# New TensorE times in a statically planned four-layer network, layer 3's priorities kept per image, and a new set of plan parameters

## The chip, the core and the metric

The kernel runs on one core of a Trainium2 chip. Time is device time in microseconds (us) for one call. The core's engines work at once, each through its own instruction queue in order: TensorE (PE in the profile) multiplies matrices, VectorE (DVE) and ScalarE (ACT) do elementwise work, and the SP queue issues DMA transfers. PEld is the weight load of TensorE. GpSimd (POOL) does next to nothing here.

## What is computed

The input x is 8 images of 32 channels and 256 x 256 points, float32. Four residual layers follow one another, each behind a group normalisation over 16 groups:

```
x = x + L0(gn(x))   # 1x1 convolution; a 5x5 filter per channel pooled from its result; depthwise 5x5 convolution
x = x + L1(gn(x))   # quantised 3x3 "adder" convolution: out[o] = -sum over channels and taps of |q - w[o]|
x = x + L2(gn(x))   # ordinary 3x3 convolution, 32 to 32 channels, with bias
x = x + L3(gn(x))   # 8x8 windows: layer norm, three small KAN layers summed, a fourth KAN layer, plus the window
```

A KAN layer is a layer norm, eight Gaussians `exp(-((ln - grid_k) / denom)^2)` of every element, a matrix product with them, and a second product with `silu(x)`.

Layer 1 has no product form. The kernel writes |q - w| through max(q - w, 0): for every output channel and each of the 9 taps an elementwise pass gives max(q - w, 0), TensorE sums it over channels with a matrix of constants, and a total of q over all taps, one for each half image, mends the rest.

## The kernel before

**Tasks and the plan.** The kernel is not written in the order in which it runs. `stage0` to `stage3` describe each layer of each image as tasks (`Plan.add`): an engine, an assumed duration in us, the buffers it needs, and a rank, which is its priority. `Plan.run` plays these tasks through on the host with a list scheduler: whenever an engine is free it takes the ready task of the lowest rank whose buffers fit. The order that comes out is what each engine's queue gets. On the chip that order is fixed; an engine that meets a late operand waits, and all behind it waits too. Assumed durations and ranks therefore change nothing but the order, and the buffers' allocation.

**Layer 1 as filler.** Layer 1 of an image is 32 passes (2 halves of the image, 16 groups of 2 output channels, `Pass`), each of 18 terms (2 channels, 9 taps). One term has three steps: a distance (`Parts.distance`: L1202 on DVE, or a piece of it on ACT, L1204) of 32 rows of 256 or 258 points from `qh` into a bfloat16 buffer `dv`; a gather (`Parts.gather`: 16 matmuls at L1220, called a gather below) that adds it into the PSUM tile `psA`; and the release of the `dv` buffer. There are two `dv` buffers (`NDV = 2`). In image 0 alone distances may also lie in the big `arena`. `Pass.piece` lets ACT begin a term's first `RA` rows once ACT has had no other work for `IDLE[image]` us; what is left of the term is taken by DVE or by ACT. DVE takes a distance whenever none of its ordinary tasks is ready, and a gather is urgent on PE. At the end of a pass `Parts.residual` (L1212, L1214) adds layer 1's input, loaded into the tile `xr` by SP (L1294), and the half image's total `ss`; an ACT task (L1299, the gate) empties `psA` into `xr`, ACT squares it for the next norm (L730), and SP stores it (L1310). There is one `psA`, so the next pass's gathers wait for the gate. There are `NXR` tiles `xr`.

**Totals.** A half image's total is nine PE tasks of 16 matmuls (L1226) into `psC`, an ACT copy (L1270) and a DVE subtraction (L1274) into `ss`. Their rank is the image's number minus `SUMS`.

**The other layers in between.** While image b is in layer 1, its neighbours are in layers 0, 2 and 3. Layer 0 (from image 1 on) is matmuls at L1027, evicted by ACT at L1053; layer 2 is L1378. Layer 3 works through 8 chunks an image. Most of its PE work is the helper `mm16` (L687: 16 float32 matmuls, which the trace records as 32). Its ACT work is mostly the Gaussians: a square (L1636) and an exponential (L1651), 256 of each an image; its DVE work is the scaling by the norm (L1531). Once all of layer 1 is done (`Plan.over`), DVE may take squares (L1641), evictions (L1479) and squares of the variance (L1483) from ACT. All chains of layer 3 go through one PSUM tile `psB`. `TURN` holds 14 shifts of priority for the steps of layer 3; one row serves images 0 to 6, a second one image 7. `L0A`, `L0B`, `L2A`, `L3A` and `L3B` place each image's layers in the ranks.

**Fillers at the end.** After the last layer-1 work, `spin` matmuls (L1845) fill 0.7 of each idle stretch that the plan expects on PE.

Of the kernel before, what the change touches and what calls it, by code (L numbers as in the profile page):

```python
# [29 lines left out]
GRID = 8  # L30
# [32 lines left out]
WK = KG + 5  # L63
# [8 lines left out]
TURN = (  # L72
    (0.8482, -0.3, 0.2988, 1.0831, 0.6872, 0.2653, 0.143, 0.632, 0.405, 0.4783, 0.2467, 0.4067, 0.8418, 0.3135),
    (0.8722, -0.1754, 0.2988, 0.9706, 0.6706, 0.3621, 0.0629, 0.4997, 0.7442, 0.312, 0.2568, -0.197, 0.8314, 0.3104),
)
# [7 lines left out]
URGENT = 1  # L83
NXR = 1
NXO = 2
MEM = 41280
IDLE = (8.0, 8.0, 16.0, 8.0, 8.0, 8.0, 8.0, 8.0)
NDV = 2
SPARE = 2816
WIDE_SPARE = 5632  # L90
BASE_SPARE = 0
EARLY = 0
HOLDT = 2
HOLD = 1
SUMS = 1.667
RA = 16
HALVES = 0
WARM = 0.7
PAIR = 0
SWITCH = 0.006  # L100
L0A = (0.1812, 0.5892, 0.4534, 0.6, -0.0586, 0.2257, 0.2237)
L0B = (1.2, 1.2, 1.2, 1.2, 1.2, 1.2, 1.2)
L2A = (-0.1294, 0.3683, 0.0757, 0.4, 0.3872, 0.3266, 0.371, 0.2281)
L3A = (0.6, 0.5583, 0.6, 0.5465, 0.6, 0.6, 0.3101, 0.3024)
L3B = (0.5054, 1.4107, 0.3679, 0.499, 0.4628, 1.2444, 1.3823, 0.5913)

# [33 lines left out]
class Plan:  # L140
# [7 lines left out]
    def __init__(self, room):  # L148
        self.tasks, self.passes = [], []

        self.free, self.places, at = {}, {"psA": [0], "psB": [0], "psV": [0], "psC": [0], "dv": list(range(NDV))}, 0
        for kind, n, size in room:
            if size:
                self.places[kind] = list(range(n // size))
            else:
                self.free[kind] = [(at, n)]
                at += n
        self.first_pass, self.filling = 0, False

    def add(self, eng, us, fn, r=(), w=(), rank=0.0, after=(), table=None, spare=0, kb=0, acc=(), dma=(1, 4.0)):  # L160
        t = Task()
        t.eng, t.us, t.fn, t.rank, t.table, t.spare, t.kb = eng, us, fn, rank, table, spare, kb
        t.dma = dma
        t.n, t.gate, t.other = len(self.tasks), None, None
        deps = {d for d in after}
        for b in r:
            deps.update(b.writers)
        for b in w:
            deps.update(b.writers)
            deps.update(b.readers)  # L170
        t.need = [b for b in acc if b.kind != "fixed"]
        t.bufs = list({id(b): b for b in (*r, *w, *acc)}.values())
        for b in t.bufs:
            b.left += 1
            if b.first is None:
                b.first = t
                if b.kind != "fixed" and b not in acc:
                    t.need.append(b)
        for b in acc:
            b.writers.append(t)  # L180
        for b in r:
            b.readers.append(t)
        for b in w:
            b.writers, b.readers = [t], []
        t.wait = len(deps)
        t.outs = []
        for d in deps:
            d.outs.append(t)
        t.ready, t.over = 0.0, False
        self.tasks.append(t)  # L190
        return t
# [75 lines left out]
    def run(self):  # L267
# [24 lines left out]
        while left or any(not p.done for p in self.passes):  # L292
            moved = True
            while moved:
                moved = False
                for e in engines:
# [31 lines left out]
                    if e == "PE":  # L328
                        us += 0.05 * ((t.n is None) != self.filling)
                        self.filling = t.n is None  # L330
                    if t.table in (LN_EXP, SILU):
# [5 lines left out]
                    if e == "SP":  # L337
                        at, (n, land) = now, t.dma
                        for _ in range(n):
                            at = max(at, landed.pop(0)) + us / n  # L340
                            landed.append(at + land)
                        busy[e] = at
                        mover = max(mover, now) + t.kb / self.RATE
                        t.end = max(mover, at + land)
                        landed[-1] = t.end
                    else:
                        busy[e] = t.end = now + us
                        if e == "ACT" and t.n is not None:
                            self.idle = t.end
                    heapq.heappush(events, (busy[e], 1, count, None))  # L350
                    heapq.heappush(events, (t.end, 2, count, t))
                    count += 1
# [4 lines left out]
            while events and events[0][0] <= now + 1e-9:  # L357
# [3 lines left out]
                elif what == 2:  # L361
# [4 lines left out]
                    for d in t.outs:  # L366
                        d.wait -= 1
                        lat = 0.0 if d.eng == t.eng and t.eng != "SP" else self.LAT[t.eng]
                        d.ready = max(d.ready, t.end + lat)
# [17 lines left out]
    def filler(self, eng, us, fn, need, bufs, ended):  # L387
        t = Task()
        t.eng, t.us, t.fn, t.need, t.bufs = eng, us, fn, list(need), list(bufs)
        t.n, t.table, t.kb, t.outs, t.ended, t.rank = None, None, 0, [], ended, 0.0  # L390
        return t

# [25 lines left out]
class Pass:  # L418
# [61 lines left out]
    def on_pe(self, plan, urgent):  # L480
# [4 lines left out]
        if self.queue and (len(self.queue) >= URGENT or not urgent):  # L485
            o, t, d, a, z = self.queue.pop(0)
            us, bufs, n = 0.05 + 0.22 * (-(-z // 8) - a // 8), [d], 1
            for v in range(a // 2, z // 2):
                self.rows[v % NJ] += 1
            fn = lambda: self.parts.gather(self, d, o, t, a, z)  # L490
        elif (
            not self.added and self.residual.over and self.low.over and (self.left < 6 or not urgent)
            and self.whole()
        ):
            us, bufs, n = 1.6, [self.ss], 0
            fn = lambda: self.parts.residual(self)
# [17 lines left out]
def kernel(  # L514
# [178 lines left out]
    class Norm:  # L693
# [43 lines left out]
        def finish(self):  # L737
# [4 lines left out]
            def first():  # L742
# [11 lines left out]
            plan.add(  # L754
                "PE", 0.6, lambda: nc.tensor.matmul(pv(), mat(average), self.mv, start=True, stop=True),
                r=[small], w=[p], rank=self.rank,
            )

            def second():
# [6 lines left out]
            plan.add(  # L766
                "PE", 0.6, lambda: nc.tensor.matmul(pv(), mat(average), self.d, start=True, stop=True),
                r=[small], w=[p], rank=self.rank,
# [49 lines left out]
    def stage0(b, rank, span, after):  # L818
# [40 lines left out]
        def fold():  # L859
# [5 lines left out]
        plan.add(  # L865
            "PE", 0.6, lambda: nc.tensor.matmul(psC[:, 0, 0:1], mat(W0), mr, start=True, stop=True),
            r=[sm["c0"]], w=[p], rank=r(0.2),
# [11 lines left out]
        def parts():  # L879
# [11 lines left out]
        plan.add(  # L891
            "PE", 0.6,
            lambda: nc.tensor.matmul(pk(), mat(MS), part.rearrange("p i j -> p (i j)"), start=True, stop=True),
# [8 lines left out]
        plan.add(  # L902
            "PE", 0.6, lambda: nc.tensor.matmul(pk(), mat(W0), pooled, start=True, stop=True),
            r=[sm["c1"]], w=[p], rank=r(0.2),
# [83 lines left out]
        def one_block(k, half, xo):  # L988
# [59 lines left out]
            for t in [K + mid] + [t for t in range(3 * K) if t != K + mid]:  # L1048
                plan.add("PE", 0.98, lambda t=t: taps(t), r=[xt, sm["w4"]], w=[p], acc=[xo] if t == K + mid else [], rank=rk)
            plan.add("PE", 0.8, edge, r=[sm["diag"], sm["c1"]], w=[p], rank=rk)  # L1050
            prev.append(plan.add(
# [8 lines left out]
        for k in range(NCH):  # L1060
# [63 lines left out]
            for n, t in enumerate(tap_order):  # L1124
                plan.add(
                    "PE", 1.07, lambda t=t, n=n, tap=tap: tap(t, first=(n == 0)),
                    r=[xt, sm["diag"]], w=[p], rank=rk,
# [108 lines left out]
    def stage1(b, x1buf, qbuf):  # L1236
# [3 lines left out]
        for h in range(NH):  # L1240
# [24 lines left out]
            for t in range(9):  # L1265
                plan.add(
                    "PE", 0.88, lambda h=h, t=t: Parts().total(h, t), r=qh_buf, w=[p], rank=b - SUMS
                )
# [50 lines left out]
    def stage2(b, norm, x2buf, rank, span, after):  # L1319
# [15 lines left out]
        for k in range(NCH):  # L1335
# [51 lines left out]
            for n, t in enumerate(taps):  # L1387
                plan.add(
                    "PE", 1.07, lambda t=t, n=n, tap=tap: tap(t, first=(n == 0), last=(n == 8)),
                    r=[xt, sm["w2f"]], w=[p], rank=rk,  # L1390
# [31 lines left out]
    def stage3(b, norm, x3buf, rank, span):  # L1422
        im = img[b]
        odd, turns = b % 2, TURN[b == nb - 1]
        cenf, resf = (wt[:, K0 * K0 + 3 + 2 * odd + i, :] for i in range(2))
# [3 lines left out]
        def fold():  # L1429
# [8 lines left out]
        plan.add(  # L1438
            "PE", 0.6, lambda: nc.tensor.matmul(psC[:, 0, 0:1], mat(C32), mr, start=True, stop=True),
            r=[sm["c3", odd]], w=[p], rank=r(0),  # L1440
# [24 lines left out]
        def variance(n, t, cen, bias, rk, src, sq=None):  # L1465
# [3 lines left out]
            for p, ps, i, us in parts():  # L1469
                at = slice(i * FS, (i + (2 if us < 1 else 4)) * FS)  # L1470
                plan.add("PE", 0.87 + 0.2 * us, lambda ps=ps, i=i: cen(ps(), i), r=src, w=[p], acc=[c], rank=rk, spare=SPARE)
                evict = plan.add(
# [23 lines left out]

            plan.add("PE", 1.1, var, r=[sq], acc=[v], rank=rk)
            return c
# [13 lines left out]
        def scale(n, t, c, rk):  # L1512

            rs = stat[t][1]
            for p, ps, first, us in parts():
# [11 lines left out]

                plan.add("PE", 0.87 + 0.2 * us, bc, r=[rs, c], w=[p], rank=rk)
                plan.add(
# [72 lines left out]
        def kan(n, t, at, rk):  # L1602
# [20 lines left out]
            def main(k):  # L1623
                mains.append(plan.add(
                    "PE", 1.07,
                    lambda bas=bases[k]: mm16(psB, tl[:, WK + 9 * n + k, :], spans(sb(bas)), k == 0, False, view=view),
                    r=[bases[k]], w=[acc], rank=rk,
# [76 lines left out]
            if n == 3:  # L1704
# [6 lines left out]
            plan.add(  # L1711
                "PE", 1.07, lambda: mm16(psB, tl[:, WK + 9 * n + GRID, :], src, False, not more, view=view),
                r=[si], w=[acc], rank=rk,
            )
            for m, (a, wm, s_) in enumerate(more):
                plan.add(
                    "PE", 1.07, lambda wm=wm, s_=s_, m=m: mm16(psB, wm, s_, False, m == len(more) - 1),
                    r=[a, sm["resf", odd]], w=[acc], rank=rk,
# [249 lines left out]
```

## Time and profile before

| what | us |
|---|---|
| median of 3 runs | 14098.98 |
| lowest and highest of them | 14069.48 to 14101.82 |
| the profiled execution's own time | 14074.93 |
| its span, first to last instruction | 14073.2 |
| PE, DVE, ACT busy in it | 12345.7, 12645.1, 11273.3 |
| first distance, last gather (trace) | 404.5, 12615.1 |

The span falls into four stretches by the trace: a head until about 408 us (layer 0 of image 0), image 0's layer 1 without any layer 3 beside it until about 1640 us (the last time that a distance lies in the arena), seven more images of layer 1 with the other layers beside them until 12615 us, and a tail in which layers 2 and 3 of the last images run. Matmul records overlap, so a busy PE is not a full one; DVE and ACT records of neighbouring instructions overlap by about 0.1 us, so the step from one start to the next is the better cost.

### The profile page before, as it was taken

Reading aid. Unit: us, or ns where it says so; the run is one execution under the profiler, and the core shown is the slowest. Engines: PE = TensorE matmul, PEld = TensorE weight load, DVE = VectorE, ACT = ScalarE, POOL = GpSimd, SP = SyncE. Lnnn points to the kernel's source line nnn. Section 1 sums busy time; section 2 is a strip of 40 time slices with the busy share of each in tenths; the row PEclk is TensorE's granted clock in tenths of the full one; section 3 lists DMA queues with packets and bytes.
Section 4 is the critical chain, followed back from the end, with each engine's and each line's share of the span. In section 5 each row is a group of like instructions: output and inputs, shape, how many; then the busy total and the mean of one; then the engine's idle time right before and its main releaser. Section 6 shows DMA issues by size and latency. Waiting matters only on the chain. (4 is left out here: it accounts for less than half of the span.)

```text
span 14073.2 us, 508061 instructions
## 1 busy us (share of the span) xinstructions
PE 12345.7 (88%) x237500; PEld 4097.9 (29%) x237744; DVE 12645.1 (90%) x7707; ACT 11273.3 (80%) x7526; POOL 17.3 (0%) x23
## 2 busy tenths in 40 slices
PE   6798978999899888998899988998888888788888
PEld 4232322222222222222222222222222222223333
DVE  1899899998999999998989899898999999995787
ACT  1565568898688888888888888888889879997887
POOL 0000000000000000000000000000000000000000
PEclk9898999999999999999999999999999999999999
DMA  4434365665765655656666656665554545556675
GB/s 113 109 79 110 95 160 145 152 155 143 184 152 148 159 165 138 146 144 156 175 147 150 153 149 174 158 149 153 150 132 127 137 135 136 127 136 180 167 194 152
DMA packets 2259390, 2052.63 MB, mean 146 GB/s; under 512 B 1418240, under 2 KB 1897472, under 8 KB 2168192
## 3 DMA queue, kind: packets, MB, share of 16 engines
q1 hardware_dynamic: 2257280, 2020.11, 57.0%
q8 instruction: 1860, 30.47, 0.9%
q14 instruction: 250, 2.05, 0.1%
HBM read 1247.93 MB, written 771.75 MB: 144 GB/s over the span
## 5 line engine op out<-in xcount | busy, mean ns | idle before, releaser
L1202 DVE TENSOR_SCALAR dv<-qh,w1q 128x8192 bf16<-128x8192 bf16 (+6 forms) x4922 | 10122.0, 2121 | 492.4 <-PE psA L1220 476.8
L1220 PE MATMUL psA<-dv,sel_b 128*32 128x512 bf16 x70823 | 4861.2, 389 | 816.9 <-DVE dv L1202 676.1
L1636 ACT ACTIVATE arena<-arena,kb 128x2048 f32<-128x2048 f32 x1690 | 3351.7, 1997 | 360.9 <-DVE arena L1531 250.8
L1220 PEld LDWEIGHTS <-sel_b 128*32 128x32 bf16 x73728 | 1808.7, 96 | 5272.1 <-issue 4091.0
L1651 ACT ACTIVATE arena<-arena 128x2048 f32<-128x2048 f32 x1690 | 3191.0, 1902 | 0.4
L687 PE MATMUL psB<-arena,tl 32*32 32x512 f32 x67184 | 2558.0, 610 | 274.7 <-ACT arena L1651 134.2
L1027 PE MATMUL psC<-arena,w 64*32 64x510 f32 (+2 forms) x26880 | 1779.2, 599 | 34.2 <-issue 20.8
L687 PEld LDWEIGHTS psB<-arena,tl 32*32 32x32 f32 x67184 | 668.6, 104 | 1337.3 <-issue 666.2
L1531 DVE TENSOR_TENSOR arena<-psB,arena 128x2048 f32<-128x2048 f32 (+1 forms) x298 | 662.4, 2223 | 65.8 <-PE psB L1523 64.4
L1378 PE MATMUL psB<-arena,tl 32*32 32x510 f32 (+3 forms) x16384 | 625.4, 605 | 21.4 <-issue 21.1
L1027 PEld LDWEIGHTS psC<-arena,w 64*32 64x32 f32 x26880 | 366.7, 105 | 907.1 <-issue 866.0
L1204 ACT ACTIVATE dv<-qh,w1n 128x4096 bf16<-128x4096 bf16 (+2 forms) x95 | 349.5, 3697 | 325.6 <-PE psA L1220 313.1
L687 PE MATMUL psB<-si,tl 32*32 32x512 f32 x13952 | 574.8, 607 | 21.6 <-issue 8.1
L1724 ACT ACTIVATE si<-psB,cols_sb 128x2048 f32<-128x2048 f32 x185 | 363.2, 1963 | 272.0 <-PE psB L687 268.9
L1641 DVE SCALAR_TENSOR_TENSOR arena<-arena,kb 128x2048 f32<-128x2048 f32 x234 | 538.4, 2347 | 30.7 <-PE psB L687 21.0
L1474 ACT ACTIVATE arena<-psB 128x2048 f32<-128x2048 f32 (+1 forms) x216 | 402.8, 1865 | 195.4 <-PE psB L687 194.5
L1482 ACT ACTIVATE arena<-arena 128x2048 f32<-128x2048 f32 x286 | 547.4, 1914 | 11.7 <-DMA syd<-arena 4.1
L1651 ACT ACTIVATE arena<-arena,kbsq 128x2048 f32<-128x2048 f32 x234 | 455.4, 1993 | 0.8 <-DVE arena L1641 0.8
L1523 PE MATMUL psB<-rs,tl 32*32 32x512 f32 x9248 | 353.0, 615 | 97.4 <-DVE arena L1531 62.0
L1845 PE MATMUL psA<-qh,eye_b 128*128 128x512 bf16 x1636 | 395.5, 384 | 0.0
L1491 PE MATMUL psV<-arena,tl 128*32 128x512 f32 x2560 | 349.0, 615 | 51.1 <-ACT arena L1482 31.1
L1299 ACT ACTIVATE xr<-psA,wsum 128x512 f32<-128x512 f32 x256 | 174.0, 680 | 252.1 <-PE psA L1220 235.5
(194 smaller groups left out, 7507.1 us busy)
## 6 DMA issues: line engine op xcount, KB each, us to landing
arena<-x SPq DMA_DIRECT2D x192, 1024.0 KB
arena<-in_x_dram SPq DMA_DIRECT2D x450, 384.0 KB
arena<-y SPq DMA_DIRECT2D x128, 1024.0 KB
si<-sy SPq DMA_DIRECT2D x484, 256.0 KB
arena<-in_x_dram SPq DMA_DIRECT2D x256, 256.0 KB
xr<-x SPq DMA_DIRECT2D x256, 256.0 KB
x<-xr SPq DMA_DIRECT2D x256, 256.0 KB
x<-arena SPq DMA_DIRECT2D x64, 1024.0 KB
```

The lines of the kernel that those rows point to most:

```text
L687: nc.tensor.matmul(view(o[j * C : (j + 1) * C, i - first, :]), w_, src(rows, i, j), start=start, stop=stop)
L1027: nc.tensor.matmul(o[:, :, c0:c1], w4[rows, t, :], grid(rows)[:, 2 * j + y : 2 * j + y + 2, c0 + dx : c1 + dx], start=t == K + mid, stop=F ...
L1202: nc.vector.tensor_scalar(dst, src, w1q[:, at : at + 1], 0.0, ALU.subtract, ALU.max)
L1220: nc.tensor.matmul(psA[j * C : (j + 1) * C, :], sel_b[:, w, :], v, start=start, stop=stop)
L1378: nc.tensor.matmul(o[:, lo - 2 * j : hi - 2 * j, c0:c1], (wc if t == 4 else tl[:, W2T + t, :])[rows], d[rows, lo + dy + 1 : hi + dy + 1, c ...
L1474: lambda ps=ps, at=at: nc.scalar.activation(sb(c)[:, at], ps().rearrange("p s f -> p (s f)"), func, bias=shift),
L1482: square = plan.add("ACT", 1.82, lambda: nc.scalar.activation(sb(sq), sb(c), AF.Square), r=[c], w=[sq], rank=rk)
L1531: lambda ps=ps, at=at: nc.vector.tensor_tensor(sb(c)[:, at], ps().rearrange("p s f -> p (s f)"), sb(c)[:, at], ALU.mult),
L1636: lambda: nc.scalar.activation(sb(bas), sb(rb), AF.Square, bias=kb[:, n, k : k + 1]),
L1641: nc.vector.scalar_tensor_tensor(sb(bas), sb(rb), kb2[:, n, k : k + 1], sb(rb), ALU.add, ALU.mult)
L1651: lambda: nc.scalar.activation(sb(bas), sb(bas), AF.Exp, scale=-1.0, bias=0.0 if sq.eng == "ACT" else kbsq[:, n, k : k + 1]),
L1845: nc.tensor.matmul(psA, eye_b, qh[:, 0:2, 0:W], start=True, stop=True)
```

## The change

The change has three parts, all in what the plan is fed with; no engine instruction is new.

1. PE's assumed times. A task may now have a `lap`: it is taken off when the next PE task is of the same sort (ordinary or gather), and paid when the sort changes. Tasks of 16 float32 matmuls go from 1.07 to 1.07 with a lap of 0.187, layer 0's from 0.98 to 1.013 with 0.137, a gather of 32 rows from 0.05 + 4 x 0.22 to 0.113 + 4 x 0.216 with 0.105; the fixed 0.05 for a change of sort goes.
2. `TURN` has one row for each image.
3. New values: `NXR` 1 to 2, `IDLE`, `RA` 16 to 4, `SUMS`, `HOLDT`, `SPARE`, `WIDE_SPARE`, `SWITCH`, and all of `TURN`, `L0A` to `L3B`.

```diff
 TURN = (
-    (0.8482, -0.3, 0.2988, 1.0831, 0.6872, 0.2653, 0.143, 0.632, 0.405, 0.4783, 0.2467, 0.4067, 0.8418, 0.3135),
-    (0.8722, -0.1754, 0.2988, 0.9706, 0.6706, 0.3621, 0.0629, 0.4997, 0.7442, 0.312, 0.2568, -0.197, 0.8314, 0.3104),
+    (0.4936, -0.3, -0.0877, 0.9919, 0.4488, -0.3, 0.0124, 1.5, 0.1463, 0.6118, 0.5329, 0.0977, 0.7248, 0.4639),
...
+    (0.4384, -0.3, 0.1294, 0.698, 1.5, -0.1148, 0.0001, 0.581, 0.1183, 0.4505, 0.1448, 0.1669, 0.602, 0.3026),
 )
-NXR = 1
+NXR = 2
-IDLE = (8.0, 8.0, 16.0, 8.0, 8.0, 8.0, 8.0, 8.0)
+IDLE = (2.0, 16.0, 2.0, 8.0, 8.0, 1000.0, 8.0, 0.5)
-SPARE = 2816
-WIDE_SPARE = 5632
+SPARE = 3584
+WIDE_SPARE = 6656
-HOLDT = 2
+HOLDT = 1
-SUMS = 1.667
-RA = 16
+SUMS = 1.405
+RA = 4
-SWITCH = 0.006
-L0A = (0.1812, 0.5892, 0.4534, 0.6, -0.0586, 0.2257, 0.2237)
...
+SWITCH = 0
+L0A = (0.3978, -0.0952, -0.2956, -0.2968, -0.4814, -0.5, -0.4469)
...
                     if e == "PE":
-                        us += 0.05 * ((t.n is None) != self.filling)
-                        self.filling = t.n is None
+                        us += self.lap * ((t.n is None) != self.filling)
+                        self.filling, self.lap = t.n is None, t.lap
...
-                        busy[e] = t.end = now + us
+                        t.end = now + us
+                        busy[e] = t.end - t.lap
...
-            us, bufs, n = 0.05 + 0.22 * (-(-z // 8) - a // 8), [d], 1
+            us, bufs, n = 0.113 + 0.216 * (-(-z // 8) - a // 8), [d], 1
...
-                plan.add("PE", 0.98, lambda t=t: taps(t), r=[xt, sm["w4"]], w=[p], acc=[xo] if t == K + mid else [], rank=rk)
+                plan.add("PE", 1.013, lambda t=t: taps(t), lap=0.137, r=[xt, sm["w4"]], w=[p], acc=[xo] if t == K + mid else [], rank=rk)
...
-    odd, turns = b % 2, TURN[b == nb - 1]
+    odd, turns = b % 2, TURN[b]
```

## The prediction

> **What bounds the kernel now.** I read the page first: DVE is the busiest engine (90%), PE and ACT follow. An average over stages says little, so next came the busy times by stretch, then DVE's waits in the longest stretch, then the timeline where the waits are large.
>
> From the page, the span, the busy row and the costliest group:
>
> ```profile
> span 14073.2 us, 508061 instructions
> PE 12345.7 (88%) x237500; PEld 4097.9 (29%) x237744; DVE 12645.1 (90%) x7707; ACT 11273.3 (80%) x7526; POOL 17.3 (0%) x23
> L1202 DVE TENSOR_SCALAR dv<-qh,w1q 128x8192 bf16<-128x8192 bf16 (+6 forms) x4922 | 10122.0, 2121 | 492.4 <-PE psA L1220 476.8
> ```
>
> Distances alone are 10122 us of DVE. Busy by stretch (length, then PE, PEld, DVE, ACT, POOL, granted clock, DMA share, GB/s):
>
> ```profile
> 408.00:1640.00 1232.00, 1104.87 (x17680) 366.86 (x17706) 1218.87 (x817) 740.91 (x434) 4.58 (x2) 0.95 0.38 90
> 1640.00:12615.00 10975.00, 9714.78 (x189416) 3039.87 (x189625) 10271.52 (x6063) 9260.62 (x6308) 11.45 (x13) 0.98 0.59 149
> 12615.00:14073.00 1458.00, 1282.45 (x23434) 518.03 (x23422) 1078.90 (x600) 1197.82 (x722) 0.00 (x0) 0.98 0.67 175
> ```
>
> In image 0's layer 1 DVE is idle for 13 us of 1232: it is the bound, and ACT has 491 us to spare. In the seven images after it DVE is idle for 703 us of 10975 (6.4%), ACT for 1714. In the tail no engine is full; a chain of DVE, ACT, PE and `psB` sets the time. So before 12615 us a microsecond less of DVE work, or of DVE waiting, is about a microsecond less of time. What DVE waits for between 1640 and 12615 us (us in total, times, longest):
>
> ```profile
> DVE dv L1202 <- PE psA L1220: 474.1, 486, 22.9
> DVE ss L1274 <- ACT ss L1270: 71.4, 9, 25.2
> DVE tiny L723 <- ACT xr L1299: 54.9, 18, 24.5
> ```
>
> The first row is the pair of `dv` buffers: a distance waits until a gather has freed one. What held the gather shows in the timeline, at two places. At 8914 us (start, us, engine):
>
> ```profile
> 8913.78 2.35 DVE L1202 TENSOR_SCALAR dv<-qh,w1q 128x8192 bf16<-128x8192 bf16 x1
> 8931.06 0.69 DVE L1274 TENSOR_TENSOR ss<-psC,ss 128x512 bf16<-128x512 f32 x1 [14.94 <-ACT ss L1270]
> 8939.35 6.91 DVE L1202 TENSOR_SCALAR dv<-qh,w1q 128x8256 bf16<-128x8256 bf16 x3 [7.60 <-PE psA L1220]
> ...
> 8922.02 8.37 PE L1226 MATMUL psC<-qh,sel_b 128*32 128x512 bf16 x144
> ```
>
> All nine tasks of a total run as one block of 8.37 us, and DVE stands for 22.5 us: first at the subtraction behind it, then for a buffer. At 9394 us:
>
> ```profile
> 9416.71 9.18 DVE L1202 TENSOR_SCALAR dv<-qh,w1q 128x8256 bf16<-128x8256 bf16 x4 [22.88 <-PE psA L1220]
> ...
> 9401.79 0.68 SPq L1294 DMA_DIRECT2D xr<-x  x1
> ...
> 9412.17 1.12 PE L1212 MATMUL psA<-xr,mats_sb 128*128 128x512 f32 x2 [2.14 <-DMA xr<-x]
> ```
>
> The pass cannot close before its `xr` has landed, no gather of the next pass can run, and DVE stands for 22.9 us. There is one `xr`.
>
> **The change, part by part.**
>
> *Less distance work on DVE.* In the timeline at 900 us distances start 2.26 us apart for 8192 points and 1.19 for 4096, so one of n points costs 0.13 + 0.00026 n us. In the compiled order of both kernels DVE's distances fall from 5116 to 5037 and their points (for each partition) from 37,143,328 to 36,831,052; ACT's pieces rise from 172 to 361, points from 703,712 to 1,015,988. DVE saves 312,276 x 0.00026 + 79 x 0.13 = 81 + 10 = 91 us. Of the points 188,912 (49 us) leave in image 0, where DVE is 99% busy; 88,956 leave in image 2 and 62,072 in image 7; the others take a few back. All of it lies before 12615 us.
>
> What ACT gains: the trace has 3584 points at 3285 ns and 4096 at 3709, so 0.83 ns a point and, start to start, a fixed 0.2 us. 312,276 x 0.00083 + 189 x 0.2 = 297 us, of which 178 in image 0, where 491 are idle. The cover is that idle time; if it is gone, each us on ACT delays squares and exponentials, on which `psB`'s PE tasks wait. After image 0 ACT goes from 84% to about 85%. The ACT pieces of 1024 points (`RA = 4`) are not in this trace: from the rows 0.2 + 0.85 = 1.05 us; bounds 0.9 and 1.3.
>
> [...] The row gives DVE a fixed 0.13 us an instruction. [...]
>
> *Totals.* Before, six of the 14 totals after image 0 run as a block of eight or nine tasks; DVE's gaps from a total's first matmul to 9 us past its last are 31.8, 11.0, 7.6, 9.4, 14.5 and 22.5 us, 97 in all. The eight that are strewn between gathers have 25 us, 3.1 each. After, by the compiled order, none behind image 0 has more than three tasks in a row, and they start 1 to 8 terms into their half instead of 2 to 18. Six at 3.1: 97 - 19 = 78 us saved. What is late next is the subtraction L1274 itself, if ACT's copy comes late; that is in the 3.1.
>
> *Residuals.* With `NXR = 2` SP's queue has two loads of `xr` ahead of a store, where before load and store strictly alternate; the number of DMAs hardly changes (2398 to 2396 rows). PE's stretches without a gather around a residual that exceed 4 us (0.88 us a task) fall from 22 to 11 of 222, and their excess from 141 to 9 us. PE's waits for `xr` were 52 us (37 times); the DVE gaps beside them, outside the totals, add up to 38 us. I take the 38.
>
> *PE's assumed times.* The trace around 6005 us: a gather and an ordinary task alternate at 2.05 us the pair (0.98 and 1.07), and four L1027 in a row take 3.6, so 0.88 to 0.90 each. The old plan assumed 2.10 and, in a row, 1.07 or 0.98; the new one gives 2.05 and 0.88. This moves no cost by itself. Stretches of PE between gathers over 3.5 us, after image 0, lose 113 of 163 us of excess; that is totals and residuals again, so not counted twice. Two tasks between gathers become commoner (566 to 900 times), about 1.9 us, under one distance of 2.26. Bounds: -60 to +60 us, taken at 0.
>
> *Tail.* PE's tasks behind the last gather are the same in number. DVE gives 20 squares back (-45), takes 10 squares of the variance (+22) and 13 evictions (+16); ACT the reverse: -7 and +7 us. Spins go from 1636 to 2037, as ordinary tasks in a row are now shorter in the plan. Order alone moves it: 0, bounds -40 to +60. Head: one image, one chain, 0.
>
> Sum on the profiled execution: 14073 - 91 - 78 - 38 = 13866. The median lies 26 above the span (14098.98 against 14073.2): 13892, rounded to 13890 (-1.5%).
>
> **The rivals.** A difference of 0.3% (42 us) is about what a measurement of this kernel can tell from no change.
>
> 1. *Only the work goes, the waits come back.* A wait that ends at one place opens at the next: of 474 us of buffer waits, 199 have a pause of PE beside them that nothing in the trace explains (for instance 1.71 us inside a task at 6026 us), and no order removes those. Then only the 91 us count: 14099 - 91 = 14008. For it: 318 of the 486 buffer waits average 0.63 us and are tied to no block. Against: the large ones have named causes, and these are gone from the order.
> 2. *The small waits go too.* 200 us of buffer waits (318 times) have no pause of PE beside them: the plan thought gathers free the buffer earlier than they do, and the new times are closer. Half of it: 13890 - 100 = 13790.
> 3. *Slower: no slack left against PE's pauses.* The old plan's long PE times were a reserve: where ordinary tasks run in a row it thought each 0.18 us longer than it is, so PE ran ahead of it and caught up after a pause. The true times take the reserve away, and with two `dv` buffers each pause reaches DVE. If buffer waits grew from 474 to 800 us: 13890 + 326 = 14216. It decides from about 680 us of such waits on (474 + 207). Against: PE now waits 676 us for distances, so slack is there whatever the plan assumes.
> 4. *ACT becomes the bound.* 119 us more on ACT after image 0, in images 2 and 7, ahead of exponentials; with half of it passed on, 13950.
>
> **How the numbers follow.** The sum as worked out, within 13830 to 13960 (ACT's rival inside): 0.58. Rival 1, 13960 to 14060: 0.18. Rival 2, below 13830: 0.10. Rival 3: 0.14, a fourth of it within 0.3%. Under 14057 is "faster": 0.58 + 0.17 + 0.10 = 0.85, less 0.05 for a tail at its upper bound on top of rival 1: 0.80. Within 0.3%: 0.08. Slower by more: 0.12. The range leaves out half of rival 2's chance and most of rival 3's: 13770 to 14110.
>
> **What would show it.** Right: `dv` L1202's count near 5037 with about 91 us less; idle DVE before the last gather down from 717 to about 600 us; the wait of L1274 for L1270 under 25 us; PE's wait for `xr` near 0; no L1226 block of 8 us; last gather near 12408 us, tail still near 1458. Wrong: buffer waits above 680 us, ACT over 90% in images 2 or 7 with PE's waits for L1651 up, or a tail over 1520.

## The result and the profile after

The changed kernel is a little slower where 1.5% less time was forecast: 14120.89 us median of 8 runs (14099.37 to 14151.44) against 14083.35 us of the kernel before (8 runs; the first three of them had a median of 14098.98), ratio 1.0026, 95% interval 1.0017 to 1.0036. The profiled execution took 14099.37 us, the fastest of its eight, with a span of 14097.6.

From the page of the changed kernel, the span, the busy row and the distances. DVE is 65 us less busy than before (12580.4 against 12645.1) and the span is 24 us longer, so DVE stood idle for 89 us more.

```profile
span 14097.6 us, 509350 instructions
PE 12419.1 (88%) x238145; PEld 4160.6 (30%) x238145; DVE 12580.4 (89%) x7631; ACT 11579.0 (82%) x7714; POOL 14.9 (0%) x23
L1210 DVE TENSOR_SCALAR dv<-qh,w1q 128x8192 bf16<-128x8192 bf16 (+8 forms) x4864 | 10040.5, 2122 | 620.1 <-PE psA L1228 585.6
```

The same stretches as before: image 0's layer 1, the seven images after it, the tail (length, then PE, PEld, DVE, ACT, POOL, granted clock, DMA share, GB/s):

```profile
403.00:1581.00 1178.00, 1080.59 (x17470) 373.31 (x17466) 1166.21 (x755) 912.64 (x539) 2.27 (x2) 0.95 0.39 93
1581.00:12543.00 10962.00, 9716.10 (x189874) 3083.67 (x189862) 10264.29 (x6050) 9381.32 (x6393) 11.37 (x13) 0.97 0.59 149
12543.00:14097.00 1554.00, 1375.80 (x23823) 531.91 (x23823) 1076.88 (x603) 1209.39 (x722) 0.00 (x0) 0.98 0.65 164
```

Image 0 ends near 1579 us instead of 1641: a gain of 62 us, 5 of them in the head. The seven images take 10962 us; before they took 10972 from the same point. The tail takes 1555 us instead of 1458. So in these two traces 72 us were gained up to the last gather (12543 against 12615) and 97 lost behind it.

The line numbers of the changed kernel stand 7 or 8 higher: L1210 is the distance, L1228 the gather, L695 the helper `mm16`, L1035 layer 0. DVE's waits in the seven images (us in total, times, longest):

```profile
DVE dv L1210 <- PE psA L1228: 584.1, 727, 7.0
DVE tiny L731 <- ACT xr L1307: 18.7, 9, 9.5
...
DVE ss L1282 <- ACT ss L1278: 8.8, 1, 8.8
```

The waits that stood out before have shrunk: the total's subtraction from 71.4 to 8.8 us, the wait for the gate's tile from 54.9 to 18.7, and the longest buffer wait from 22.9 to 7.0. But the buffer waits have grown from 474.1 us in 486 to 584.1 us in 727: many small ones took the place of few large ones. I sorted them by the PE work that stood between the gather that released the buffer and the gather before that one. Behind about 2 us of such work there were 131 waits with 97 us before, and now there are 417 with 235 us. (Sorted only by the time between the two gathers, 1.75 to 2.95 us, it is 150 with 99 us and 397 with 225 us.) The rest of the buffer waits fell a little.

A place where this happens, from the timeline of the changed kernel at 6037 us, right behind the residual that closes a pass (L1220, L1222), PE and then DVE:

```profile
6034.51 1.05 PE L1228 MATMUL psA<-dv,sel_b 128*32 128x512 bf16 x16
6035.48 1.12 PE L1220 MATMUL psA<-xr,mats_sb 128*128 128x512 f32 x2
6036.44 0.59 PE L1222 MATMUL psA<-ss,eye_b 128*128 128x512 bf16 x2
6036.97 1.05 PE L1228 MATMUL psA<-dv,sel_b 128*32 128x512 bf16 x16
6037.95 2.35 PE L695 MATMUL psB<-arena,tl 32*32 32x512 f32 x64
6040.23 1.05 PE L1228 MATMUL psA<-dv,sel_b 128*32 128x512 bf16 x16
6041.21 1.14 PE L695 MATMUL psB<-si,tl 32*32 32x512 f32 x32
6042.28 1.05 PE L1228 MATMUL psA<-dv,sel_b 128*32 128x512 bf16 x16
...
6041.34 6.88 DVE L1210 TENSOR_SCALAR dv<-qh,w1q 128x8192 bf16<-128x8192 bf16 x3 [0.60 <-PE psA L1228]
```

Two tasks of `mm16` (64 matmul records) lie between two gathers, which start 3.26 us apart; around the residual it was 2.46 us. A distance needs a buffer every 2.26 us, so the two cycles come 1.20 us late together, and DVE stands for 0.60 us. With one task in between, gathers start 2.05 us apart (6040.23 to 6042.28), and DVE does not wait.

Over the whole trace, where PE had no pause over 0.1 us from one gather of 32 rows to the next, the medians are:

| between two gathers | start to start, us (cases) | old plan, us | new plan, us |
|---|---|---|---|
| nothing | 0.87 (373) | 0.93 | 0.87 |
| one `mm16` | 2.05 (678) | 2.10 | 2.05 |
| two `mm16` | 3.26 (194) | 3.17 | 2.93 |
| three `mm16` | 4.31 (11) | 4.24 | 3.81 |
| one `mm16`, one L1035, in this order | 3.12 (132) | 3.08 | 2.87 |
| two L1035 | 2.85 (175) | 2.99 | 2.87 |

The new assumed times are right for one task, and for layer 0's in a row. For a second float32 task of `mm16` they are 0.33 us too short, where the old ones were 0.09 short; for an `mm16` with a layer 0 task behind it they are 0.25 short.

The change also shortens five other assumed times, which the list of its parts leaves out: the small matmuls of the norms and folds (0.6 to 0.35), layer 0's edges (0.8 to 0.5), the sums for the variance (1.1 to 0.87), the residual (1.6 to 1.49) and a task of a total (0.88 to 0.87). Where the trace has clean cycles for them, they are not too short: 2.47 us for a residual and a gather where the new plan has 2.47 (120 cases), 1.74 for a sum for the variance where it has 1.85 (94), 1.29 for edges where it has 1.48 (13).

### The profile page after: what moved, and what is told of

Read it like the earlier page. It is cut to its first block, busy times and chain, and to the rows that moved or that the text cites. A ratio compares the mean times of both kernels' runs of the same rounds, so it can differ in the third digit from the quotient of the medians.

```text
span 14097.6 us, 509350 instructions
## 1 busy us (share of the span) xinstructions
PE 12419.1 (88%) x238145; PEld 4160.6 (30%) x238145; DVE 12580.4 (89%) x7631; ACT 11579.0 (82%) x7714; POOL 14.9 (0%) x23
## 5 line engine op out<-in xcount | busy, mean ns | idle before, releaser
L1210 DVE TENSOR_SCALAR dv<-qh,w1q 128x8192 bf16<-128x8192 bf16 (+8 forms) x4864 | 10040.5, 2122 | 620.1 <-PE psA L1228 585.6
L1228 PE MATMUL psA<-dv,sel_b 128*32 128x512 bf16 x70394 | 4844.9, 390 | 873.0 <-DVE dv L1210 752.6
L1228 PEld LDWEIGHTS <-sel_b 128*32 128x32 bf16 x73728 | 1818.2, 96 | 5175.7 <-issue 3982.9
L695 PE MATMUL psB<-arena,tl 32*32 32x512 f32 x65984 | 2501.9, 613 | 215.2 <-ACT arena L1658 106.4
L1035 PE MATMUL psC<-arena,w 64*32 64x510 f32 (+2 forms) x26880 | 1746.2, 596 | 6.4 <-issue 5.2
L695 PEld LDWEIGHTS psB<-arena,tl 32*32 32x32 f32 x65984 | 654.4, 104 | 1258.8 <-issue 658.2
L1212 ACT ACTIVATE dv<-qh,w1n 128x1024 bf16<-128x1024 bf16 (+3 forms) x211 | 501.4, 2402 | 242.5 <-PE psA L1228 233.2
L1035 PEld LDWEIGHTS psC<-arena,w 64*32 64x32 f32 x26880 | 379.0, 105 | 913.9 <-issue 884.3
L695 PE MATMUL psB<-si,tl 32*32 32x512 f32 x14048 | 570.4, 605 | 35.6 <-issue 15.8
L1482 ACT ACTIVATE arena<-psB 128x2048 f32<-128x2048 f32 x213 | 398.7, 1872 | 157.4 <-PE psB L695 156.3
L1852 PE MATMUL psA<-qh,eye_b 128*128 128x512 bf16 x2037 | 493.6, 381 | 0.0
L1212 ACT ACTIVATE arena<-qh,w1n 128x1024 bf16<-128x1024 bf16 (+3 forms) x150 | 436.6, 2961 | 69.1 <-PE psA L1228 69.0
L1648 DVE SCALAR_TENSOR_TENSOR arena<-arena,kb 128x2048 f32<-128x2048 f32 x195 | 448.0, 2346 | 12.0 <-PE psB L695 10.4
L1658 ACT ACTIVATE arena<-arena,kbsq 128x2048 f32<-128x2048 f32 x195 | 377.8, 1989 | 0.8 <-DVE arena L1648 0.8
```

What stands on the lines that cost most here:

```text
L695: nc.tensor.matmul(view(o[j * C : (j + 1) * C, i - first, :]), w_, src(rows, i, j), start=start, stop=stop)
L1035: nc.tensor.matmul(o[:, :, c0:c1], w4[rows, t, :], grid(rows)[:, 2 * j + y : 2 * j + y + 2, c0 + dx : c1 + dx], start=t == K + mid, stop=F ...
L1210: nc.vector.tensor_scalar(dst, src, w1q[:, at : at + 1], 0.0, ALU.subtract, ALU.max)
L1212: nc.scalar.activation(dst, src, AF.Relu, bias=w1n[:, at : at + 1])
L1228: nc.tensor.matmul(psA[j * C : (j + 1) * C, :], sel_b[:, w, :], v, start=start, stop=stop)
L1648: nc.vector.scalar_tensor_tensor(sb(bas), sb(rb), kb2[:, n, k : k + 1], sb(rb), ALU.add, ALU.mult)
```

## The experiments

**The new times alone.** Theory A: the plan fails by the times of float32 tasks (of `mm16`) in a row. Theory B: the new priorities are worse. The values before do not give a plan under the new times, as the plan runs out of room for buffers; with `TURN` and `L3A` shifted by at most 0.03 each they give one under the old times and under the new. `pair_old` is the first, the control; `pair_new` has the same values and all of the new times.

```diff
 pair_old against before
-TURN = (
-    (0.8482, -0.3, 0.2988, 1.0831, 0.6872, 0.2653, 0.143, 0.632, 0.405, 0.4783, 0.2467, 0.4067, 0.8418, 0.3135),
...
+TURN = ((0.833, -0.2951, 0.3271, 1.0926, 0.6862, 0.2538, 0.1213, 0.6619, 0.4203, 0.4633, 0.2524, 0.4192, 0.8662, 0.3003), (0.861, -0.1942, 0.3042, 0.9959, 0.6847, 0.3405, 0.0552, 0.4743, 0.7239, 0.3116, 0.236, -0.2108, 0.816, 0.3057))
...
-L3A = (0.6, 0.5583, 0.6, 0.5465, 0.6, 0.6, 0.3101, 0.3024)
+L3A = (0.6213, 0.5424, 0.6068, 0.5405, 0.5875, 0.5879, 0.3268, 0.323)
```

> The kernel before with its TURN and L3A values shifted by at most 0.03 each, so that the same values also give a plan with the new PE times (the next run); it is the control of that run. Both theories: within 1% of before, 14080 to 14220 us, small waits on dv buffers as before (about 130 waits behind 2 us of other PE work, about 100 us).

Measured: 14120.23 us, ratio to before 1.0019 (1.0010 to 1.0028). Buffer waits are 518 us in 508, those behind about 2 us of PE work 99 us in 133, the last gather 12643, the tail 1476. The control is close to the kernel before, as expected. But its 36 us over before (14083.98 beside it), from shifts of at most 0.03, are as much as the whole change made of the time (38 us): a result of this size says little about single values.

```diff
 pair_new against pair_old
-                        us += 0.05 * ((t.n is None) != self.filling)
-                        self.filling = t.n is None
+                        us += self.lap * ((t.n is None) != self.filling)
+                        self.filling, self.lap = t.n is None, t.lap
...
-            us, bufs, n = 0.05 + 0.22 * (-(-z // 8) - a // 8), [d], 1
+            us, bufs, n = 0.113 + 0.216 * (-(-z // 8) - a // 8), [d], 1
...
```

> The same values as pair_old, with the new PE times (laps) and nothing else. Theory A (the times are at fault: a float32 task in a row is assumed at 0.88 us and takes 1.05 to 1.2, so the plan puts two tasks between gathers): two-task stretches go from about 600 to about 850, waits on dv buffers behind 2 us of other PE work from about 130 to over 300, buffer waits in all up by 60 us or more, the last gather not earlier than in pair_old, the tail longer; time 30 to 150 us above pair_old. Theory B (the new priorities are at fault): buffer waits and time within 0.3% of pair_old, or less.

Measured: 14439.39 us, ratio to before 1.0248 (1.0233 to 1.0264), so 319 us or 2.3% above its control; both ran on the same chip. Of DVE's waits in the seven images, the two largest of `pair_old`, then the two largest of `pair_new` and its wait at the total's subtraction:

```profile
DVE dv L1199 <- PE psA L1217: 518.2, 508, 22.4
DVE ss L1271 <- ACT ss L1267: 68.9, 9, 24.8
```

```profile
DVE dv L1201 <- PE psA L1219: 765.6, 776, 32.3
DVE tiny L722 <- ACT xr L1298: 101.4, 17, 36.7
...
DVE ss L1273 <- ACT ss L1269: 0.9, 2, 0.5
```

The buffer waits rise by 247 us, of which 149 behind about 2 us of PE work (133 to 410 waits, 99 to 248 us). The last gather moves from 12643 to 12917 us, and the tail grows from 1476 to 1519. In the plan, stretches of two tasks between gathers go from 604 to 853. Theory A holds in its direction, at over twice the price that I had given it; theory B does not, as the values did not change and the loss is larger than that of the whole change.

How much of the loss is the second task is less sure. The run has all the new times at once, those of the short tasks too, and the waits behind about 2 us of work are 149 us of the 319; the other buffer waits grew by 98 us, and DVE's wait for the gate's tile grew from 60.2 to 101.4 us. A run with the rows of `mm16` put right and the other new times kept was not made. Why the new times make the plan put two tasks between gathers more often was not tried either.

The new times also do good, and the prediction did not know it. The wait at the total's subtraction falls from 68.9 to 0.9 us, and DVE's gaps around the fourteen totals behind image 0 from 116 to 52 us, though `SUMS` is the old one. So the totals are broken up by the new times alone, and the 319 us are what is left of the loss after this gain.

The pair says more. With the same new times, the changed kernel's median is 14120.89 us and that of `pair_new` 14439.39. So the new values as a whole are worth about 319 us under the new times. In the two traces it is 338 us (spans of 14097.6 and 14436.0): 375 us before the last gather, less 36 in the tail. The change is a gain of about that size and a loss of nearly the same size. What the new values would give under the old times was not run; the next section says why the two cannot simply be added.

**The tail without spins.** The tail grew by 97 us while the spins went from 1636 to 2037. Theory C: they stand in PE's way. Theory D: the order of the tail is worse.

```diff
-WARM = 0.7
+WARM = 0.0
```

> The changed kernel without the spin matmuls (WARM = 0): same order of everything else. Theory C (the tail's 97 us come from 401 more spins, placed in idle time that does not exist because rows of tasks take longer than planned): the tail falls from 1555 to about 1470 us, time near 14035. Theory D (the tail's order is worse, or rows of tasks simply take longer): the tail stays over 1530 us, or grows if a slower TensorE clock follows from the idle time; the granted clock in the tail falls from 0.98.

Measured: 14143.77 us, ratio to before 1.0038 (1.0025 to 1.0051). The tail of `after_nospin`, in the columns used above:

```profile
12582.00:14158.00 1576.00, 1053.55 (x21786) 396.04 (x21754) 1077.35 (x603) 1209.09 (x721) 0.00 (x0) 0.78 0.63 161
```

The tail grows to 1577 us instead of falling to 1470. But the granted clock in it falls from 0.98 to 0.78, so the run changes two things at once: it takes away the spins' delay, if there was one, and it runs at a lower clock. Theory C is not borne out; that spins cost nothing is not shown.

The run tells one thing more. DVE's order is the same as in the changed kernel, yet the seven images took 10996 us in this trace, with 619 us of buffer waits, against 10962 and 584 there. So some 35 us between two single traces carry no meaning. Of the 72 us gained up to the last gather only those of image 0 come back in each of the three traces with this order up to the tail (this one, the changed kernel's and the next run's; image 0 ends at 1580 to 1585 us, the last gather is at 12543 to 12581); the rise of 247 us in the pair is far larger.

**The tail with the old row of priorities.** Image 7's layer 3 lies wholly in the tail.

```diff
-    (0.4384, -0.3, 0.1294, 0.698, 1.5, -0.1148, 0.0001, 0.581, 0.1183, 0.4505, 0.1448, 0.1669, 0.602, 0.3026),
+    (0.8722, -0.1754, 0.2988, 0.9706, 0.6706, 0.3621, 0.0629, 0.4997, 0.7442, 0.312, 0.2568, -0.197, 0.8314, 0.3104),
```

> The changed kernel with the old row of TURN for image 7, whose layer 3 lies wholly in the tail. Theory D (the tail's order by the new row is worse): the tail falls from 1555 to about 1460 to 1500 us, time 14020 to 14070, and the last gather stays within 10 us of 12543. Theory C (spins) or theory A (rows of tasks): the tail stays at 1540 or above.

Measured: 14147.11 us, ratio to before 1.0046 (1.0029 to 1.0062). The last gather is at 12547 us and the tail 1590 us long, 35 longer than with the new row. The new row is not what lengthens the tail. Of the 97 us, the pair shows 43 for the new times, with the old values; the other 54 may lie in values that were not tried one by one (`HOLDT`, `SPARE`, the last places of `L2A`, `L3A`, `L3B`), or in how these and the times act together. This stays open.

## Why the prediction was wrong

*The step that failed* is "PE's assumed times". It said that this part "moves no cost by itself", and that two tasks between gathers are "about 1.9 us, under one distance of 2.26". Both halves were wrong. I had taken the time in a row from four tasks of L1027, a layer-0 task, and carried it over to tasks of `mm16`, the most frequent sort of ordinary task (2816 of them, 1680 of layer 0). And I set only the two tasks against the distance, without the gather that follows them: the buffer comes free once in a whole cycle, and two tasks and a gather take 2.85 to 3.26 us. The trace of the kernel before had it. In the timeline that I read it stands 16 us behind the four L1027, between two gathers 3.12 us apart:

```profile
6020.59 1.05 PE L1220 MATMUL psA<-dv,sel_b 128*32 128x512 bf16 x16
6021.57 1.14 PE L687 MATMUL psB<-arena,tl 32*32 32x512 f32 x32
6022.64 1.14 PE L1027 MATMUL psC<-arena,w 64*32 64x510 f32 x16
6023.71 1.05 PE L1220 MATMUL psA<-dv,sel_b 128*32 128x512 bf16 x16
```

I had counted the two-task stretches (566 to 900) and priced them at 0 within 60; behind them lie about 138 us more of waits in the changed kernel. The new times alone cost 319 us with the old values.

The forecast span was 13866 us and the measured one is 14097.6, so 232 us are to be accounted for. Of these, 135 lie before the last gather (forecast at 12408 us, measured at 12543), where the growth of the small buffer waits stands. The other 97 are the tail, a second term that was put at 0: +97 against bounds of -40 to +60. I had reasoned from loads, and loads hardly changed (DVE 1078.9 to 1076.9 us, ACT 1197.8 to 1209.4); what lengthened the tail is open for the larger part.

*Why the plan was misled.* Inside a row, the records of `mm16` do start 0.88 us apart, but only in the first step or two. In the tail of the kernel before, later steps are mostly 1.04 to 1.06 us, and the work behind a row starts later still: of the 3.26 us with two tasks, 0.98 go from the gather to the first task, 0.88 to the second, and 1.39 to the next gather. The steps at the head of a row therefore make a task look shorter than it is. The new lap of 0.187 fits the first step and misses what is paid at the end of the row.

*Distance work*: right in the count (5037), and right for image 0. Its end came 62 us earlier, 56 of them behind the head, for 49 expected from its points; DVE's busy time on distances fell there by 57 us (1143.1 to 1085.7). In the seven images it fell by 5 us only (9290.1 to 9285.2), where the points that left (312,276 less the 188,912 of image 0, at 0.00026 us) are worth 32.

*Totals and residuals*: nearly right in size. DVE's gaps around the fourteen totals behind image 0 fell from 122 to 52 us, so by 70 where 78 were forecast. But the pair brings a like gain by the new times alone, which the prediction put at nothing: this term was read off the finished order, without knowing what had made it. PE's waits for `xr` at the residual fell from 52.0 us in 37 to 8.2 us in 10; with one `xr` and the new times (`pair_new`) they are 36.3 us. These gains are real, and were spent on the small buffer waits: in the seven images DVE's idle time is 698 us, against 703 before.

*Busy time in the seven images* hardly fell (10268.6 to 10264.3 us) though distances left it. Most of the difference can be worked out: records of neighbouring instructions overlap by about 0.1 us (2.35 us long, 2.26 us apart); each new wait breaks one overlap, and 241 more buffer waits make, by this estimate, about 22 us. A wait costs 0.09 us (2.35 less 2.26) more than its gap shows.

*Rivals.* Rival 3 came nearest, and it was right that the new times can cost more than they bring. But its ground is not what the cycles show. It took the old plan's rows to be 0.18 us a task too long; for two `mm16` the old plan was 0.09 short, and only layer 0's rows had such a reserve (2.99 against 2.85). Buffer waits with an unexplained pause of PE beside them cost less than before (about 127 us against 199), and all buffer waits of the changed kernel ended at 584 us, short of the 680 from which this rival was to decide. In `pair_new` they passed it (766), so that the lost reserve of layer 0 has a part in that run is not excluded. ACT took the added work in its idle time, at 86% of the seven images.

With the new values the new times do less harm: buffer waits of 584 us against 766 in `pair_new`. So the gain of about 319 us under the new times is no measure of what these values bring under others. Values found under times that are right for rows of float32 tasks too would be the version to try; none was run.

## What to carry to other kernels

In a planned kernel an assumed duration is part of the schedule: making the model truer for one pattern and falser for another can cost as much as new priorities gain (here about 319 us each). Take a task's time for a row from whole cycles, from one fixed point to the next behind the row, for each sort of task, and not from the steps between starts (here 1.21 us for the second `mm16`, where the step was 0.88). And price a stretch of other work by the full cycle of the resource that waits, with the step that frees it.

## What the runs showed that was not expected

By whole cycles, a second task of `mm16` (sixteen 32 x 32 tiles) is no cheaper than the first. A gather behind a gather starts 0.87 us later; one, two and three `mm16` between them make it 2.05, 3.26 and 4.31, so they add 1.18, 1.21 and 1.05 us, though the first three start 0.88 us apart. One, two and three layer 0 tasks of 64 rows make it 1.99, 2.85 and 3.70: they add 1.12, 0.86 and 0.85. Why the two sorts differ was not tried. Without spins, which are work that nobody reads, the granted TensorE clock of the tail is 0.78 instead of 0.98. The call's median is then 23 us higher (14143.77 against 14120.89); but the intervals of the two ratios to before overlap (1.0025 to 1.0051 and 1.0017 to 1.0036), so that this is a cost of the slower clock is not shown.
